# A two-layer graph network on one core: the first layer's sort with fp32 messages, summed one-hots and contiguous operands, and x + offset kept in DRAM

## Chip, core and metric

The kernel runs on one core of one Trainium2 chip. The metric is the device time of one execution in microseconds (us). The core's engines are TensorE (PE; its weight loads are shown apart, as PEld), VectorE (DVE), ScalarE (ACT), GpSimd (POOL) and SyncE (SP, which here only issues DMAs). Each works through its own instruction queue in order and waits there on semaphores.

## What is computed

12,500 nodes with 256 features, 200,000 edges (src, dst) sorted by dst, one weight per edge. Layer 0 is an attention layer with 4 heads of 32, layer 1 a message-passing layer; each is followed by a residual and a layer norm.

```
feat      = relu(x @ W + b)                    # two projections: self (4x32), neighbour (4x32)
att_s     = leaky(feat_self . a_self);  att_n = leaky(feat_nei . a_neigh)
msg[e]    = (att_s[src] + att_n[dst]) * weight[e] * feat_nei[dst]
agg       = segment_sum(msg, src)
norm      = per head (32 wide): (f - mean) * scale * rsqrt(var) + offset,  for self and for agg
x1        = layernorm(x + concat(norm(self), norm(agg)))
m[e]      = relu(concat(x1[src], x1[dst]) @ W_msg + b_msg);  agg1 = segment_sum(m, dst)
h         = layernorm(relu(concat(x1, agg1) @ W_upd + b_upd)) * gamma + beta
out       = layernorm(x1 + h)
```

## The kernel before

Three stages follow one another. **Stage 1, the sort** (tasks in `sort_tasks` and `feat_tasks`), takes the edges in 112 groups of 14 tiles of 128. The dst of a group lie in a window of 128 nodes, whose neighbour features are computed beside it; the messages have to be ordered by blocks of 128 src nodes (98 blocks, and one for padding). For a group:

- `hot` (L530, DVE) makes a one-hot A of each edge's block, laid out block by tile; `ranks` (L550, PE) sums it over edges with 14 products of one column, `begins` (L562) makes the prefix over edges with 14 products; `rows`, `shift`, `steps` and `target` (L605) turn the counts into places in the log and row addresses (`reach` builds Z, whose weights `target` reads at every fourth column).
- `place_mm` (L591, L593, PE) lays each edge's place beside a large constant at its block, in three pieces of 5, 5 and 4 tiles; `place_max` (L617, DVE) reduces each to the maximum over blocks, `split` makes row and column of the place, `hot_r`, `hot_q` (DVE) and `goods` (L637, POOL) their one-hots times four values of the edge, and `permute` (L648, PE) orders these with 14 products.
- `rel_keep`, `rel_out`, `rel_in` send the ordered window positions through DRAM and back broadcast to 128 partitions (512 KB), `hot_n` (L668, DVE) makes one-hots of them, and `message` (L677, PE) multiplies these with the features. Since the one-hots are bf16, the features are split into three bf16 parts (`high`, `rest`, `mid`, `low3`) and each product is done three times: 48 a group. `evict` (L684, ACT) copies them out and `scatter` (L690, POOL) writes 4 x 128 rows to the log in DRAM.
- `feat_tasks` also normalises the self half and adds it to x + offset for one block a group. The result stays in SBUF: the low half transposed (`low_t`, L491; yl), the high half as it is (yh), with statistics of the low half (`low_stats`).

**Stage 2** takes the 98 src blocks in turn. Five pieces of the log a block (`log_load`, SP) are scaled by the attention (`log_hot`, L888, four on POOL and one on DVE), and DVE makes 20 one-hots of the src node times the edge weight (L893) from iotac, a ramp in SBUF; PE sums (`log_sum`, L901, 20 products). For batches of four blocks (`spans`) the head norm follows, then the sum with yh, the layer norm's statistics and the projection for layer 1 (`proj_t` to `proj_s`), which goes to DRAM as pd.

**Stage 3** takes the edges in 781 steps of two tiles: POOL gathers rows of pd by src (L1204), PE adds the window's projection (L1241), DVE and ACT form the sum and the relu (L1263, L1265), PE sums by dst (L1282), and per group the update and the norms follow. `store_x1` (L793) writes x1 of a block to DRAM from yl and yh, one block a group.

The order of each engine's instructions is the order in which the program issues them (PE, ACT, DVE and SP are scheduled by hand; POOL's by the framework). In stage 1 a group begins every 8 steps, and each task stands in a list with its step from the group's begin; at each step the tasks due are issued, older groups first. So four groups are under way at once. A tile of a pool has as many buffers as its `bufs` says (2 where none is given for most pools of stage 1), and a writer waits until the reader of its buffer is done.

Of the kernel before, what the change touches and what calls it, by code (L numbers as in the profile page):

```python
# [29 lines left out]
H = 4  # L30
# [51 lines left out]
def kernel(  # L82
# [43 lines left out]
    pd = dram.tile([ROWS, D], FT, name="pd")  # L126

# [11 lines left out]
    yl = consts.tile([P, NB, P], FT, name="yl")  # L139
    yh = consts.tile([P, NB, HD], FT, name="yh")  # L140
    bst = consts.tile([P, NB, 2, 6], FT, name="bst")
# [57 lines left out]
    with ExitStack() as l0:  # L199
        dcp = l0.enter_context(tc.tile_pool(name="dcp", bufs=1))  # L200
        meta = l0.enter_context(tc.tile_pool(name="meta", bufs=2))
        xin = l0.enter_context(tc.tile_pool(name="xin", bufs=3))
        feat = l0.enter_context(tc.tile_pool(name="feat", bufs=2))
        srt = l0.enter_context(tc.tile_pool(name="srt", bufs=2))
        msgp = l0.enter_context(tc.tile_pool(name="msgp", bufs=2))
# [4 lines left out]
        iotab = dcp.tile([P, NBX, GT], BF, name="iotab")  # L210
# [11 lines left out]
        roww = dcp.tile([P, RW], FT, name="roww")  # L222
        quart = dcp.tile([P, 1], FT, name="quart")
# [3 lines left out]
        nc.gpsimd.iota(iotaw, pattern=[[1, GR]], base=0, channel_multiplier=0,  # L227
# [12 lines left out]
        nc.vector.tensor_copy(iotab, iotac[:, 0:NBX, None].to_broadcast([P, NBX, GT]))  # L240
# [103 lines left out]
        def rel_group(g):  # L344
            c, j = divmod(g, GC)
            n = ntile[g]
            sl = slice(g * GT, g * GT + n)
            nc.vector.tensor_scalar(rel[:, sl], rel[:, sl], baseB[:, g:g + 1], None, op0=OP.subtract)
            nc.vector.tensor_single_scalar(em[c][:, 0, j * GT:j * GT + n], rel[:, sl], 1.0, op=OP.add)

# [16 lines left out]
        def feat_tasks(g):  # L367
# [22 lines left out]
            def keep():  # L390
                xT = feat.tile([P, 4, P], FT, name="xT", bufs=1)
                a, z = (0 if ww else 2), (4 if bb else 2)
                nc.scalar.copy(xT[:, a:z].rearrange("p c q -> p (c q)"), st["tp"][:, a * P:z * P])
                st["xT"] = xT

            def offsets():
                st["y"] = feat.tile([P, HD], FT, name="y")
                nc.vector.tensor_tensor(st["y"], xb[g][:, 0:HD], ofb[:, 0:HD], op=OP.add)
                nc.vector.tensor_tensor(yh[:, g, :], xb[g][:, HD:D], ofb[:, HD:D], op=OP.add)
# [18 lines left out]
            def att_mult():  # L418
                st["tm"] = feat.tile([P, D], FT, name="tm", bufs=1)
# [11 lines left out]
            def centre():  # L431
                st["F"] = feat.tile([P, D + H], FT, name="F")
# [13 lines left out]
            def square():  # L446
                st["q"] = feat.tile([P, HD], FT, name="q", bufs=1)
                nc.scalar.activation(st["q"], st["F"][:, 0:HD], AF.Square)


            def high():
                F3[g] = feat.tile([P, 3, HD + H], BF, name="F3")
                nc.scalar.copy(F3[g][:, 0], st["F"][:, HD:])

            def rest():
                st["r"] = feat.tile([P, HD + H], FT, name="r", bufs=1)
                nc.vector.tensor_tensor(st["r"], st["F"][:, HD:], F3[g][:, 0], op=OP.subtract)

            def mid():
                nc.scalar.copy(F3[g][:, 1], st["r"])  # L460

            def low3():
                nc.vector.tensor_tensor(F3[g][:, 2], st["r"], F3[g][:, 1], op=OP.subtract)
# [19 lines left out]
            def put():  # L483
                nc.vector.tensor_tensor(st["y"], st["y"], st["F"][:, 0:HD], op=OP.add)

            def low_stats():
                nc.vector.bn_stats(bst[:, g, 0], st["y"])

            def low_t():
                st["yt"] = ps.tile([P, 512], FT, name="tp")  # L490
                nc.tensor.transpose(st["yt"][:, :P], st["y"], ident)  # L491

            def low():
                nc.scalar.copy(yl[:, g, :], st["yt"][:, :P])
# [5 lines left out]
                    (11, k(square)), (12, w(high)), (12, k(var)), (13, w(rest)), (13, k(root)), (14, w(mid)),  # L500
                    (14, k(rstd)), (14, k(norm)), (15, w(low3)), (15, k(scale)), (15, k(put)),
                    (16, k(low_stats)), (16, k(low_t)), (17, k(low)))
# [13 lines left out]
        def sort_tasks(g):  # L516
# [10 lines left out]

            def hot():
                st["A"] = srt.tile([P, NBX, GT], BF, name="A")
                nc.vector.tensor_tensor(st["A"], iotab, blk[c][:, None, tl].to_broadcast([P, NBX, GT]),  # L530
                                        op=OP.is_equal)

            def twins():
                e = srt.tile([P, GT, GT], BF, name="e", bufs=1)
# [10 lines left out]
            def ranks():  # L545
# [3 lines left out]
                for t in range(GT):  # L549
                    nc.tensor.matmul(st["sm"][:NBX, 0:1], st["A"][:, :, t], onesb,  # L550
                                     start=(t == 0), stop=(t == GT - 1))
# [6 lines left out]
            def begins():  # L558
                r = st["rows"]
                nc.tensor.matmul(st["sm"][:NBX, 1:2], less[:NBX, :NBX], r, start=True, stop=True)  # L560
                for t in range(GT):
                    nc.tensor.matmul(st["V"], lessb, st["A"][:, :, t], start=(t == 0), stop=False)  # L562
# [19 lines left out]
            def reach():  # L582
                nc.vector.tensor_scalar(small("Z", GR, bufs=1), iotaw[:NBX], st["b0"], None, op0=OP.is_ge)

            def place_mm(i):
                def f():
# [6 lines left out]
                    nc.tensor.matmul(o, identk, st["A"][:, :, a:a + n].rearrange("p b t -> p t b"),  # L593
# [9 lines left out]
            def target():  # L603
                for k in range(RW):
                    nc.tensor.matmul(st["sm"][:, 4 + k:5 + k],  # L605
                                     st["Z"].rearrange("b (p k) -> b k p", k=RW)[:, k], st["ds"],
# [5 lines left out]
            def place_max(i):  # L612
                def f():
                    a, n = CH[i]
                    if i == 0:
                        small("sl", GT, p=P)
                    nc.vector.tensor_reduce(  # L617
                        st["sl"][:, a:a + n], st.pop(("w", i))[:, :n * NBX].rearrange("p (t b) -> p t b", b=NBX),
                        AX.X, OP.max)
                return f  # L620

            def split():
                sl = st["sl"]
                q, r, f = small("q", GT, BF, p=P), small("r", GT, BF, p=P), small("f", GT, p=P)
                nc.vector.scalar_tensor_tensor(sl, sl, -BIG, st["d"], op0=OP.add, op1=OP.add)
# [4 lines left out]
            def hot_r():  # L630
                st["rh"] = srt.tile([P, NR, GT], BF, name="rh", bufs=1)
# [3 lines left out]
            def goods():  # L635
                st["mv"] = srt.tile([P, NR, 5, GT], BF, name="mv", bufs=1)
                nc.gpsimd.tensor_tensor(st["mv"], st["rh"][:, :, None, :].to_broadcast([P, NR, 5, GT]),  # L637
                                        em[c][:, None, :, tl].to_broadcast([P, NR, 5, GT]), op=OP.mult)

            def hot_q():  # L640
                st["qh"] = srt.tile([P, P, GT], BF, name="qh", bufs=1)
# [3 lines left out]
            def permute():  # L645
                mv = st["mv"].rearrange("p r m t -> p (r m) t")
                for t in range(GT):
                    nc.tensor.matmul(st["sm"][:, 16:16 + 5 * NR], st["qh"][:, :, t], mv[:, :, t],  # L648
# [18 lines left out]
            def hot_n():  # L667
                nc.vector.tensor_scalar(st["rr"], st["rr"], pcol1, None, op0=OP.is_equal)  # L668
                st["oT"] = st["rr"].rearrange("p (q r) -> p q r", r=NR)

            def message(i):
                def f():
                    r0, n = 3 * i, min(3, NR - 3 * i)
                    mp = st["mp", i] = ps.tile([P, 512], FT, name="mp")
                    for r in range(n):
                        for k in range(3):
                            nc.tensor.matmul(mp[:, r * (HD + H):(r + 1) * (HD + H)], st["oT"][:, :, r0 + r],  # L677
                                             F3[g][:, k], start=(k == 0), stop=(k == 2))
# [9 lines left out]
            def scatter(k):  # L688
                def f():
# [7 lines left out]
                    for p in zeros[-16:] if g >= GZ else zeros[:nz0] if g < 2 else []:  # L697
# [3 lines left out]
            tasks = [(0, lambda: rel_group(g)), (0, hot), (0, twins), (1, ranks), (2, rows), (2, twin_sum),  # L701
                     (3, begins), (4, vhigh), (5, vlow), (5, shift), (5, reach), (6, place_mm(0)), (6, place_mm(1)),
                     (6, steps), (7, place_max(0)), (7, steps_keep), (8, place_max(1)), (8, place_mm(2)),
# [835 lines left out]
```

## Time and profile before

| | us |
|---|---|
| three runs, lowest, median, highest | 5433.82, 5439.74, 5442.79 |
| profiled execution, time | 5431.22 |
| its span, first to last instruction | 5429.4 |
| stage 1, stage 2, stage 3 (of the span) | 0 to 2356, to 3408, to the end |
| busy: PE, weight loads, DVE, ACT, POOL | 4904.7, 4013.7, 3925.2, 1960.4, 2885.6 |
| mean granted clock of TensorE | 0.827 of full speed |

The profile is that of one execution. It gives each engine's busy time (matmuls are pipelined and their ends are modelled, so a busy PE is not a PE at its peak), groups of instructions by source line, a timeline, and for any stretch the clock that TensorE was granted, as a share of full speed. Durations of neighbours on an engine overlap; what an instruction costs its engine is better read from the step between two starts.

### The profile page before, as it was taken

To read this page: it belongs to the slowest core of one execution; us is meant where nothing else is said; L and a number is where in the kernel's file an instruction comes from. 1 tells how busy PE (TensorE), PEld (TensorE's weight loads), DVE (VectorE), ACT (ScalarE), POOL (GpSimd) and SP (SyncE) were. 2 spreads that over 40 slices of the span, in tenths; PEclk is the share of its full clock that TensorE was granted. 3 is DMA by queue.
4 is the path that set the end of the run, shared out by engine and by line. 5 is a ranking of instruction groups with operands and counts; after the bars stand their busy time and mean duration, and the time that the engine had idled before them with its cause. 6 is when DMAs were issued, how large, how long until landed. Compare 5 with 4: busy or idle time off the path is not lost.

```text
span 5429.4 us, 85561 instructions
## 1 busy us (share of the span) xinstructions
PE 4904.7 (90%) x26835; PEld 4013.7 (74%) x26835; DVE 3925.2 (72%) x11063; ACT 1960.4 (36%) x5351; POOL 2885.6 (53%) x2797
## 2 busy tenths in 40 slices
PE   8999999999999999989999999788888888888887
PEld 6777777777777777767777777666667667676665
DVE  6767777666666676579999999666666666666666
ACT  2222222222222222211111111566666666666655
POOL 2333333333333333344544444677777777777776
PEclk7666666666666666689999999999999999999999
DMA  3333333322232222244444445566666666666665
GB/s 111 112 121 114 124 119 114 117 94 93 91 98 87 96 88 90 82 130 134 137 135 135 135 136 142 158 180 175 180 178 176 180 178 177 180 174 181 176 171 139
DMA packets 439071, 738.09 MB, mean 136 GB/s; under 512 B 85828, under 2 KB 272998, under 8 KB 438614
## 3 DMA queue, kind: packets, MB, share of 16 engines
q1 hardware_dynamic: 307878, 388.95, 24.9%
q0 software_dynamic: 110848, 327.87, 19.7%
q10 hardware_dynamic: 19888, 15.74, 0.9%
q8 instruction: 218, 3.57, 0.3%
q14 instruction: 239, 1.96, 0.1%
HBM read 540.59 MB, written 191.70 MB: 135 GB/s over the span
## 4 chain that ended last, share of the span: by engine, by line
PE 54%; DVE 21%; DMA 14%; issue 5%; ACT 3%; POOL 2%; DVEq 0%; POOLq 0%; SPq 0%; ACTq 0%
DMA gb<-pd,srcf 14%; PE sum L901 11%; PE mp L677 7%; PE agg L1282 6%; DVE rr L668 5%; PE wp L593 5%; DVE o L893 4%; PE fs L648 4%; PE wp L591 4%; PE fs L605 3%; PE qp L1241 3%; DVE gb L1263 2%; PE fs L405 2%; ACT gb L1265 2%; POOL gb L1204 2%
## 5 line engine op out<-in xcount | busy, mean ns | idle before, releaser
L1204 POOL DMA_INDIRECT gb<-pd,srcf x1563 | 1508.2, 965 | 500.4 <-issue 225.5
L690 POOL DMA_INDIRECT log<-m,ix x448 | 455.9, 1018 | 1430.9 <-ACT m L684 736.3
L1263 DVE TENSOR_TENSOR gb<-qp,gb 128x512 f32<-128x512 f32 x781 | 538.8, 690 | 661.8 <-DMA gb<-pd,srcf 519.0
L1282 PE MATMUL agg<-gb,o 128*128 128x256 f32 x3126 | 877.8, 405 | 125.6 <-ACT gb L1265 120.6
L901 PE MATMUL sum<-lg,o 120*128 120x256 f32 (+1 forms) x3920 | 918.0, 387 | 68.8 <-DVE o L893 56.1
L901 PEld LDWEIGHTS sum<-lg,o 120*128 120x128 f32 (+1 forms) x3920 | 739.0, 192 | 215.5 <-DVE o L893 91.0
L893 DVE TENSOR_SCALAR o<-iotac,lg 120x128 f32<-120x128 f32 (+1 forms) x1960 | 802.3, 478 | 48.0 <-PE sum L901 34.3
L1282 PEld LDWEIGHTS agg<-gb,o 128*128 128x128 f32 x3126 | 586.1, 198 | 315.3 <-ACT gb L1265 239.9
L1265 ACT ACTIVATE gb<-gb 128x512 f32<-128x512 f32 x781 | 490.4, 628 | 727.2 <-DVE gb L1263 724.1
L888 POOL TENSOR_TENSOR lg<-lg 120x512 f32<-120x512 f32 x392 | 449.1, 1152 | 483.3 <-DMA lg<-log 246.9
L677 PE MATMUL mp<-F,rr 128*128 128x132 bf16 x5376 | 569.9, 271 | 44.6 <-DVE rr L668 39.2
L677 PEld LDWEIGHTS <-rr 128*128 128x128 bf16 x5376 | 532.3, 163 | 66.5 <-DVE rr L668 57.8
L1241 PE MATMUL qp<-qh,oT 128*128 128x256 f32 x1563 | 550.4, 373 | 7.3 <-DMA dr<-in_dst_dram 7.3
L684 ACT COPY m<-mp 128x396 f32<-128x396 f32 (+1 forms) x672 | 303.8, 453 | 698.4 <-PE mp L677 698.2
L1241 PE MATMUL qp<-ql,oT 128*128 128x256 f32 x1563 | 415.1, 287 | 0.0
L593 PE MATMUL wp<-A,identk 128*128 128x495 bf16 x336 | 335.4, 998 | 0.0
L1241 PEld LDWEIGHTS qp<-qh,oT 128*128 128x128 f32 x1563 | 308.4, 197 | 32.0 <-DVE oT L1228 7.5
L1241 PEld LDWEIGHTS qp<-ql,oT 128*128 128x128 f32 x1563 | 308.9, 198 | 17.9
L668 DVE TENSOR_SCALAR rr<-rr,pcol 128x2048 bf16<-128x2048 bf16 x112 | 316.5, 2826 | 5.3 <-DMA rr<-reld 5.3
L617 DVE TENSOR_REDUCE sl<-wp 128x5 f32<-128x495 f32 x336 | 212.5, 632 | 137.7 <-PE wp L593 137.7
L562 PE MATMUL fs<-A,lessb 128*128 128x99 bf16 x1568 | 299.1, 357 | 0.0
L831 PE MATMUL qm<-wms,xT 128*128 128x256 f32 x224 | 90.4, 490 | 227.2 <-ACT xT L826 227.0
(244 smaller groups left out, 8616.4 us busy)
## 6 DMA issues: line engine op xcount, KB each, us to landing
dr<-in_dst_dram SPq DMA_DIRECT2D x781, 128.0 KB
lg<-log SPq DMA_DIRECT2D x392, 251.2 KB
rr<-reld SPq DMA_DIRECT2D x112, 512.0 KB
log<-zero SPq DMA_DIRECT2D x101, 268.0 KB
lg<-log SPq DMA_DIRECT2D x98, 268.0 KB
gb<-pd,srcf POOLq DMA_INDIRECT x1563, 4.0
xw<-in_x_dram SPq DMA_DIRECT2D x112, 128.0 KB
xw<-x1d SPq DMA_DIRECT2D x112, 128.0 KB
```

The lines of the kernel that those rows point to most:

```text
L593: nc.tensor.matmul(o, identk, st["A"][:, :, a:a + n].rearrange("p b t -> p t b"), start=False, stop=True)
L668: nc.vector.tensor_scalar(st["rr"], st["rr"], pcol1, None, op0=OP.is_equal)
L677: nc.tensor.matmul(mp[:, r * (HD + H):(r + 1) * (HD + H)], st["oT"][:, :, r0 + r], F3[g][:, k], start=(k == 0), stop=(k == 2))
L690: ins = nc.gpsimd.indirect_dma_start(out=log[:, :], out_offset=bass.IndirectOffsetOnAxis(ap=st["ix"][:, k:k + 1], axis=0), in_=st["m"][:, ...
L888: e.tensor_tensor(t[:n, 1, :, 0:HD].rearrange("p r (h k) -> p r h k", h=H), t[:n, 0, :, 0:HD].rearrange("p r (h k) -> p r h k", h=H), t[:n ...
L893: nc.vector.tensor_scalar(o[:n, r], iotac[:n], t[:n, 0, r, MW - 2:MW - 1], t[:n, 0, r, MW - 1:MW], op0=OP.is_equal, op1=OP.mult)
L901: nc.tensor.matmul(sums[b], o[:n, r], t[:n, :, r, 0:HD], start=(k == 0 and r == 0), stop=(k == NK - 1 and r == RW - 1))
L1204: nc.gpsimd.indirect_dma_start(out=gb[s][:r, i], out_offset=None, in_=pd[:, :], in_offset=bass.IndirectOffsetOnAxis(ap=srci[:r, t:t + 1], ...
L1241: nc.tensor.matmul(qp[:r, i], oT[:, i * P:i * P + r], q, start=(k == 0), stop=(k == 1))
L1263: nc.vector.tensor_tensor(z, qp, z, op=OP.add)
L1265: nc.scalar.activation(z, z, AF.Relu)
L1282: nc.tensor.matmul(agg[g], o[:r, i], z[:r, i], start=(j == 0 and i == 0), stop=lastmm)
```

## The change

In stage 1:
- The one-hot A is laid out tile by block, from a copy of the block numbers that ACT widens first (`widen`); DVE adds its 14 tiles to 4 (`halves`, C), and `ranks` and `begins` use C with 4 products each. `place_mm` reads A contiguously.
- `place_max` goes from DVE to ACT: 14 activations a group, relu of the value less the constant, summed over blocks by the activation's accumulator.
- `reach` fills Z so that `target` reads contiguous weights; `goods` lays mv out so that `permute` streams contiguous columns.
- `hot_n` writes fp32 one-hots to a tile of its own, and `message` is one fp32 product instead of three bf16; the split of the features goes.
- Both halves of x + offset + norm(self) go to DRAM (`out_y`, yd); the transposes, copies and statistics of stage 1 for it go.
- More buffers, and steps moved by one to three.

In stage 2 y is loaded from DRAM a batch at a time (`load_y`), the statistics are over all 256 columns, `proj_t` transposes both halves, and x1 is written here (`store_x1`, ACT and SP) instead of in stage 3. The one-hots of L893 read their ramp from PSUM (iotap), and the log is loaded 9 pieces ahead instead of 4, with 12 buffers instead of 7.

```diff
-                for t in range(GT):
-                    nc.tensor.matmul(st["sm"][:NBX, 0:1], st["A"][:, :, t], onesb,
-                                     start=(t == 0), stop=(t == GT - 1))
+                for i, v in enumerate(st["C"]):
+                    nc.tensor.matmul(st["sm"][:NBX, 0:1], v, onesb, start=(i == 0), stop=(i == 3))
...
+            def widen():
+                st["bx"] = srt.tile([P, GT, NBX], BF, name="bx")
+                nc.scalar.copy(st["bx"], blk[c][:, tl, None].to_broadcast([P, GT, NBX]))
+            def halves():
+                A = st["A"]
+                C = srt.tile([P, 7, NBX], BF, name="C")
+                nc.vector.tensor_tensor(C, A[:, 0:7], A[:, 7:14], op=OP.add)
+                nc.vector.tensor_tensor(C[:, 0:3], C[:, 0:3], C[:, 3:6], op=OP.add)
+                st["C"] = [C[:, i] for i in (0, 1, 2, 6)]
...
-                    nc.tensor.matmul(o, identk, st["A"][:, :, a:a + n].rearrange("p b t -> p t b"),
+                    nc.tensor.matmul(o, identk, st["A"][:, a:a + n],
...
-                                     st["Z"].rearrange("b (p k) -> b k p", k=RW)[:, k], st["ds"],
+                                     st["Z"][:, k * P:(k + 1) * P], st["ds"],
...
-                    nc.vector.tensor_reduce(
-                        st["sl"][:, a:a + n], st.pop(("w", i))[:, :n * NBX].rearrange("p (t b) -> p t b", b=NBX),
-                        AX.X, OP.max)
+                    w = st.pop(("w", i))
+                    for k in range(n):
+                        nc.scalar.activation(small("junk", NBX, BF, p=P), w[:, k * NBX:(k + 1) * NBX], AF.Relu,
+                                             bias=nbig, accum_out=st["sl"][:, a + k:a + k + 1])
...
-                st["mv"] = srt.tile([P, NR, 5, GT], BF, name="mv", bufs=1)
+                st["mv"] = srt.tile([P, GT, NR, 5], BF, name="mv")
...
-                nc.vector.tensor_scalar(st["rr"], st["rr"], pcol1, None, op0=OP.is_equal)
+                oT = srt.tile([P, P * NR], FT, name="oT")
+                nc.vector.tensor_scalar(oT, st["rr"], pcol1, None, op0=OP.is_equal)
...
-                        for k in range(3):
-                            nc.tensor.matmul(mp[:, r * (HD + H):(r + 1) * (HD + H)], st["oT"][:, :, r0 + r],
-                                             F3[g][:, k], start=(k == 0), stop=(k == 2))
+                        nc.tensor.matmul(mp[:, r * (HD + H):(r + 1) * (HD + H)], st["oT"][:, :, r0 + r],
+                                         F3[g][:, HD:], start=True, stop=True)
...
+            def out_y():
+                nc.sync.dma_start(yd[g * P:(g + 1) * P, :], st["y"])
...
+        iotap = ps.tile([P, P], FT, name="iotap", bufs=1)
+        nc.vector.tensor_copy(iotap, iotac)
...
-                nc.vector.tensor_scalar(o[:n, r], iotac[:n], t[:n, 0, r, MW - 2:MW - 1], t[:n, 0, r, MW - 1:MW],
+                nc.vector.tensor_scalar(o[:n, r], iotap[:n], t[:n, 0, r, MW - 2:MW - 1], t[:n, 0, r, MW - 1:MW],
...
+        def load_y(q):
+            b, n = spans[q]
+            ys[q] = bw.tile([P, BB, D], FT, name="y", bufs=3)
+            nc.sync.dma_start(ys[q][:, :n], yd[b * P:(b + n) * P, :].rearrange("(b p) w -> p b w", p=P))
...
-        LA = 4
+        LA = 9
```

In the step list of a group, `widen` stands at -3, `hot` and `halves` at -1 (`hot` was at 0), the last placement piece, `target`, `index` and `split` one or two later, `hot_r`, `goods`, `hot_q` at 12 (10), `permute` at 15 (13), `rel_out`, `rel_in` at 17 and 19 (15, 17), `hot_n` at 22 (20), the messages at 24 to 29 (21 to 26), their evictions one step behind, the scatters at 27 to 31 (24 to 28).

## Prediction, made before the result was known

> **What bounds the kernel now.** First the page's busy shares, then the stretches of the three stages: the sort of the first layer (0 to 2356 us), the sums over the log (to 3408), the second layer (to the end). In the answer by stretches the columns are the span of the stretch, busy time with counts of PE, weight loads, DVE, ACT and POOL, the granted clock, the DMA share and GB/s.
>
> ```profile
> PE 4904.7 (90%) x26835; PEld 4013.7 (74%) x26835; DVE 3925.2 (72%) x11063; ACT 1960.4 (36%) x5351; POOL 2885.6 (53%) x2797
> ```
>
> ```profile
> 0.00:2356.00 2356.00, 2280.27 (x14055) 1827.37 (x14055) 1602.03 (x4849) 577.21 (x1929) 869.73 (x793) 0.65 0.31 103
> 2356.00:3408.00 1052.00, 984.25 (x4390) 823.82 (x4391) 1004.89 (x2432) 131.22 (x366) 507.68 (x441) 0.97 0.48 136
> 3408.00:5429.00 2021.00, 1640.17 (x8392) 1362.47 (x8390) 1318.23 (x3783) 1251.99 (x3057) 1508.16 (x1563) 0.95 0.62 174
> ```
>
> The sort is bound by PE (97%) at a clock of 0.65; the log sums by DVE (96%) with PE right behind (94%). The second layer follows POOL: its timeline there is gathers of 0.95 us with 0.30 us between, one per 1.25 us; 1563 of them are 1954 of the 2021 us. So I read the sort by PE's timeline over one group (start us, us, engine, line; xN merges N instructions, and an fp32 product counts as two):
>
> ```profile
> 1000.50 0.87 PE L593 MATMUL wp<-A,identk 128*128 128x396 bf16 x1
> 1001.19 1.80 PE L605 MATMUL fs<-ds,Z 99*128 99x1 f32 x8
> 1002.86 0.74 PE L677 MATMUL mp<-F,rr 128*128 128x132 bf16 x9
> 1003.43 2.60 PE L550 MATMUL fs<-onesb,A 128*99 128x1 bf16 x14
> 1005.90 0.51 PE L677 MATMUL mp<-F,rr 128*128 128x132 bf16 x3
> ...
> 1007.29 2.67 PE L562 MATMUL fs<-A,lessb 128*128 128x99 bf16 x14
> ...
> 1011.85 2.27 PE L648 MATMUL fs<-mv,qh 128*128 128x80 bf16 x14
> 1013.94 1.17 PE L677 MATMUL mp<-F,rr 128*128 128x132 bf16 x9
> ...
> 1018.42 1.14 PE L405 MATMUL fs<-w0s,xT 128*128 128x128 f32 x8
> 1019.40 1.29 PE L677 MATMUL mp<-F,rr 128*128 128x132 bf16 x18
> ```
>
> From the first line to its next appearance at 1020.98 a group takes 20.48 us. I price by the step from one start to the next, since ends overlap. Two things are to be seen. An operand with a stride costs by the column: L593 streams 396 strided columns in 0.69 us, where L591 beside it streams 396 contiguous ones in 0.17; L562 takes 0.178 us for 99, L648 0.149 for 80, each 1.7 to 1.9 ns a column. And the clock, in stretches of 2 us, is 1.00 from 1018 to 1002 of the next group and 0.50 from 1004 to 1016: it falls behind L605 and L550, 22 products of one column that leave the array almost idle.
>
> **The sort, part by part (PE, us per group, at full clock).**
> - Counts (L550): 14 strided loads, 2.47, become 4 contiguous ones. L598 loads 99 contiguous columns twice in 0.13, so 4 x 0.065 = 0.26.
> - Prefix products (L562): 2.49 becomes 4 of 99 columns, 0.25 by L677's 0.57 for nine.
> - One-hot products of the placement (L593): 0.69 + 0.89 + 0.87 = 2.45 becomes 0.17 + 2 x 0.21 = 0.59.
> - Permutation (L648): 2.09 becomes 14 x 0.063 = 0.88; its weights stay strided, but L677's bf16 weights are strided too and pass at 0.063.
> - Targets (L605): 1.67 for 8 strided loads becomes 8 x 0.084 = 0.67 (L598's load scaled to 128 columns).
> - Messages: 48 bf16 products, 3.96, become 16 fp32, that is 32 instructions. Streaming 132 columns at L405's rate (0.98 us for 8 of 128) is 0.12 us or less, but their weights are fp32 and strided, and the nearest row is L605: 1.67/8 = 0.209 us a load. Taken: loads bound them, 32 x 0.209 = 6.7. From below 32 x 0.125 = 4.0 (L405's contiguous loads). From above, load and stream in series, 32 x 0.32 = 10.2. So messages get dearer, by 2.7.
> - The rest, unchanged but now at full clock: other placement products 1.18 (1.97 now), transposes 0.43 (0.85), L560 and L563 0.42 (1.31 with a wait of 0.47), L598 0.13, projection 0.98; the transpose of y goes (0.11).
>
> Sum: 6.7 + 0.26 + 0.25 + 0.59 + 1.18 + 0.88 + 0.67 + 0.43 + 0.42 + 0.13 + 0.98 = 12.5 against 20.48. The quiet run of 22 one-column products (4.1 us beside 0.57 of messages) shrinks to 12 in 0.9 us with messages between, so I take the clock as mostly full.
>
> [...]
>
> **The other engines of the sort now matter.** DVE is busy 14.4 us of a group. Away go the three maxima (L617, 1.8), the bf16 split of the messages (0.55), the statistics (0.2) and one of two adds (0.2). L668's one-hot takes 0.74 us alone but 3.49 mostly: it ends 0.55 us after POOL's L637 (2.26 us). Alone, with fp32 out, I put it between 0.74 and 2.1 (2048 elements at the 1.0 ns that lies between L617's two shapes, 666 and 565 ns for 495 and 396), at 1.2. Added: two half-sums of 693 and 297 elements, 0.7 to 1.2 by L530 (0.79 for 1386) and its double. That is 10.4 to 10.9, and 13 if one instruction still waits out L637, as a tiny one (L440) did for 2.82 us late in the sort. The new order of mv's elements changes L637's reads; I keep its price.
>
> ACT is busy 5.2 us and gains most: widening 1386 elements (L1265: 512 in 628 ns; L416: 256 in 418; so 1.3 us) and 14 activations of 99 columns that also sum. L1249, with a bias, takes 0.34 us a step for 128; the sum's readout appears nowhere, so from 0.31 (nothing for it) to 0.55 (a small ACT step of 0.24 more), taken 0.45: 6.3. Less three copies (0.8), ACT stands at 9.5 to 12.9, taken 11.5.
>
> PE 12.5, ACT 11.5, DVE up to 13, each in order, with two buffers between: this is no longer one bound. A ring shows it. The placement sums wait for PE's products; behind them in ACT's queue stand the group's rs copy (it waits for the permutation, and the trip through DRAM behind it), the steps copy, for which PE's targets wait, and the message evictions, for which PE's next message waits. By the steps above ACT reaches its first placement sums some 1.1 us later in a group than PE has them, and PE pays that at a message. With 1.4 more for DVE's waits and remaining half-clock windows I take **15.0 us a group**.
>
> SP gains one wait: the store of y (128 KB) waits for DVE's last add two steps earlier; behind it stand rr's load and the next x. rr's own trip, issue at 2344.36 to its one-hot at 2348.67 with DMA quiet, is 4.3 us plus 1.5 for the write before; seven steps of 1.9 us are there for it. DMA is at 0.31 of the sort; the same bytes and 128 KB more in 15/20.7 of the time make about 0.45. The -BIG constant, iotaw's order and the mask of the last rows are work ahead of the loop or in one group: nothing.
>
> First to last L668 is 55.4 to 2348.7, 111 steps of 20.66 us. Gain: 111 x (20.66 - 15.0) = 628 us.
>
> **The log sums.** A block takes 10.64 us. DVE's 20 one-hots (L893) average 478 ns in rows of 331 to 1427; the long ones wait out POOL's L888 (1.05).
>
> ```profile
> 2805.37 3.93 DVE L893 TENSOR_SCALAR o<-iotac,lg 120x128 f32<-120x128 f32 x4
> ```
>
> Here four take 3.93 us while POOL runs two products; free of it twelve take 4.62 with POOL busy at both ends. With the ramp in PSUM, L571's and L413's rows (99 in 0.25, 256 in 0.43, PSUM in) give 0.28 us, 20 x 0.28 = 5.6; if the lock does not mind, nothing is won. With the batch's steps DVE needs 8 to 9. PE then bounds: 40 x 0.216 (24 in 5.18) + 4 x 0.216 + two transposes 0.22 = 9.7. ACT's x1 stores and SP's y loads hide (ACT is at 12%), the x1 stores on SP with nine loads of lead behind them instead of four. I take 10.0: 98 x 0.64 = 63 us, bounds 0 and 92.
>
> **The second layer** loses, per group of 18 us, a transpose, two activations and a store beside POOL's gathers: 0 to 20 us, taken 10.
>
> **Sum** against the profiled execution (5431.2 us, span 5429.4): 5431 - 628 - 63 - 10 = **4730 us**. The runs' median is 0.16% above it; 0.2% is about what a measurement here can tell from no change.
>
> **Rivals.**
> - Full overlap: no ring, PE's floor of 12.5 and a bit: 12.9 x 111 gives 4500 us; if loads cost by column only, DVE's 13 takes over at the same place. For it: PE is fed without a break now. Against: ACT's load doubles. 0.17.
> - ACT takes over: at 0.75 us a sum, 5.2 + 14 x 0.75 = 15.7 and waits, 16.8 a group: 4930. No row bounds the readout from above. [...] 0.16.
> - Load and stream in series, or the clock still half for 13 of 20 us (since load-bound messages fill the array only half of the time): PE 16, with waits 17: 4950. 0.17.
> - Slower: a 64-byte stride of fp32 weights costs more than L605's 16-byte one. PE without messages is 5.8; break-even is at 20.66 + 73/111 = 21.3 us a group, messages 15.5, 0.485 us a load, 3.8 ns a column against 1.63. At 4.5 ns: 24.2 a group, 5750 us. The 28-byte strides of L550 and L562 (1.78, 1.80) speak against. 0.05.
> - The fewer products bring nothing, since the ring locks at the old period: 5360 us. 0.02.
>
> My forecast (4600 to 4860) has 0.43. Faster 0.94, same 0.01, slower 0.05. The range: 4490, for the floor, to 4990, for the half clock.
>
> **What would show it.** Per group: messages of 6.7 us in 32 steps of 0.209; counts 0.26; clock above 0.85 in the sort; ACT busy over 70% there; L893's long rows gone. Message steps far from 0.209, or ACT's sums far from 0.45, would make the number wrong.

## The result and the profile after

The changed kernel takes **4726.06 us** (median of 4 runs, 4723.41 to 4726.86) where the kernel before takes 5438.06 us (4 runs on the same chip, 5433.82 to 5442.79): ratio **0.869, 95% interval 0.8675 to 0.8705**. The forecast was 4730 us. The profiled execution's span is 4724.1 us, 705.3 less than before.

First the page's line of busy shares, then the answer by stretches for the sort (first to last `hot_n`, L659), the log sums (first to last sum, L876) and the second layer, in the columns explained above.

```profile
PE 4094.3 (87%) x22705; PEld 3495.8 (74%) x22705; DVE 3744.7 (79%) x10534; ACT 2522.8 (53%) x8179; POOL 3062.8 (65%) x2797
```

```profile
46.00:1727.00 1681.00, 1493.19 (x9759) 1338.15 (x9759) 1545.46 (x4180) 1113.76 (x4751) 1046.14 (x766) 0.95 0.44 147
1746.00:2697.00 951.00, 950.98 (x4478) 826.24 (x4478) 834.97 (x2429) 192.71 (x450) 482.61 (x439) 1.00 0.63 174
2712.00:4724.00 2012.00, 1604.10 (x8256) 1296.77 (x8256) 1316.51 (x3757) 1178.83 (x2849) 1510.84 (x1563) 0.98 0.62 169
```

The clock of the sort rose from 0.65 to 0.95, and the engine that is nearly always busy is no longer PE (89%) but DVE (1545 of 1681, 92%). In the log sums PE has taken DVE's place at 100%. The second layer is as it was, paced by POOL.

| us | before | after | gain | forecast |
|---|---|---|---|---|
| sort, per group (111 steps between first and last `hot_n`) | 20.66 | 15.14 | 5.52 | 5.66 |
| sort | 2293.3 | 1681.1 | 612 | 628 |
| log sums, per block (98) | 10.63 | 9.70 | 0.93 | 0.64 |
| log sums | 1042 | 951 | 91 | 63 |
| second layer | 2008 | 2012 | -4 | 10 |

The rest of the 705 us is the start, 9 us shorter up to the first `hot_n`, less 3 us in the gaps between the stages.

Now one group. This is the changed kernel's PE timeline; the bracket at a line's end is PE's idle time ahead of it and what the profile holds to have ended it.

```profile
1000.82 1.94 PE L667 MATMUL mp<-F,oT 128*128 128x132 f32 x8
1002.60 0.37 PE L578 MATMUL wp<-vh,identb 128*128 128x495 bf16 x1
...
1003.65 0.37 PE L580 MATMUL wp<-A,identk 128*128 128x495 bf16 x1
1005.47 0.30 PE L585 MATMUL fs<-dl,step 99*99 99x1 f32 x2 [1.45 <-ACT junk L606]
...
1007.53 2.86 PE L667 MATMUL mp<-F,oT 128*128 128x132 f32 x12
1010.23 0.33 PE L578 MATMUL wp<-vh,identb 128*128 128x396 bf16 x1
```

From step to step the twelve message instructions take 2.70 us, 0.225 each; 32 of them are some 7.1 us a group. PE's only large pause is ahead of the steps product L585. Over the whole sort it comes to 142 us, by the list of waits (us in total, times, longest), while the page's group of the messages has 4.2 us of idle time:

```profile
PE fs L585 <- ACT junk L606: 94.6, 65, 1.5
...
PE fs L585 <- DVE dl L563: 47.3, 36, 1.9
```

```profile
L667 PE MATMUL mp<-F,oT 128*128 128x132 f32 x3584 | 880.2, 394 | 4.2 <-DVE v L459 1.4
```

The name of ScalarE's placement sums (L606) misleads. L585 reads dl (DVE, `shift`), and in all 103 pauses of over 0.1 us that the sort's records have ahead of it, it starts 0.145 to 0.147 us after the end of L563, which writes dl. DVE's and POOL's timelines show why dl was late.

```profile
1001.54 0.15 DVE L562 TENSOR_TENSOR dl<-pos,b 99x1 f32<-99x1 f32 x1
1001.72 3.60 DVE L563 TENSOR_TENSOR dl<-dl,capc 99x1 f32<-99x1 f32 x1
1005.25 0.15 DVE L564 TENSOR_TENSOR pos<-pos,rows 99x1 f32<-99x1 f32 x1
```

```profile
1002.21 3.09 POOL L625 TENSOR_TENSOR mv<-rh,em 128x1120 bf16<-128x1120 bf16 x1
```

An addition of one column takes 3.60 us instead of 0.15, and it ends as POOL's goods product L625 does (1005.30). In other groups L562 is the one that waits; of the 108 runs of the two lines that take over 0.5 us, 107 end 14 to 29 ns after an L625. Over the sort the two lines take some 3.2 us a group more than their shortest; so much of DVE's 13.9 busy us is, by this reading, a wait for POOL, and the experiments have to show it.

### The profile page after: what moved, and what is told of

Same layout as the page of the kernel before. It is cut to its first block, busy times and chain, and to the rows that moved or that the text cites. A ratio compares the mean times of both kernels' runs of the same rounds, so it can differ in the third digit from the quotient of the medians.

```text
span 4724.1 us, 79669 instructions
## 1 busy us (share of the span) xinstructions
PE 4094.3 (87%) x22705; PEld 3495.8 (74%) x22705; DVE 3744.7 (79%) x10534; ACT 2522.8 (53%) x8179; POOL 3062.8 (65%) x2797
## 4 chain that ended last, share of the span: by engine, by line
PE 45%; DVE 23%; DMA 17%; ACT 7%; issue 5%; POOL 4%; DVEq 0%; SPq 0%; ACTq 0%; POOLq 0%
PE sum L876 18%; DMA gb<-pd,srcf 16%; PE mp L667 8%; PE agg L1274 5%; DVE dl L563 4%; POOL gb L1196 4%; DVE gb L1255 3%; DVE dl L562 3%; ACT gb L1257 3%; DVE oT L659 2%; PE qp L1233 2%; PE fs L592 2%; PE qm L964 2%; DVE A L512 1%; DVE Z L570 1%
## 5 line engine op out<-in xcount | busy, mean ns | idle before, releaser
L680 POOL DMA_INDIRECT log<-m,ix x448 | 520.1, 1161 | 623.4 <-ACT m L674 332.9
L876 PE MATMUL sum<-lg,o 120*128 120x256 f32 (+1 forms) x3920 | 880.2, 378 | 9.8 <-POOL lg L863 9.8
L667 PE MATMUL mp<-F,oT 128*128 128x132 f32 x3584 | 880.2, 394 | 4.2 <-DVE v L459 1.4
L667 PEld LDWEIGHTS mp<-F,oT 128*128 128x128 f32 x3584 | 819.5, 311 | 8.3 <-ACT m L674 2.2
L876 PEld LDWEIGHTS sum<-lg,o 120*128 120x128 f32 (+1 forms) x3920 | 733.0, 189 | 114.2 <-POOL lg L863 10.0
L868 DVE TENSOR_SCALAR o<-iotap,lg 120x128 f32<-120x128 f32 (+1 forms) x1960 | 656.4, 400 | 115.6 <-PE sum L876 107.7
L606 ACT ACTIVATE junk<-wp,nbig 128x99 bf16<-128x99 f32 x1568 | 520.7, 359 | 11.6 <-PE wp L580 3.3
L625 POOL TENSOR_TENSOR mv<-rh,em 128x1120 bf16<-128x1120 bf16 x112 | 355.6, 3175 | 6.6 <-DVE rh L620 3.7
L606 ACT ACTIVATION_READ_ACCUMULATOR junk<-wp,nbig 128x1 f32 x1568 | 342.1, 218 | 0.0
L1220 DVE TENSOR_SCALAR oT<-dr,baseP 128x256 fp32r<-128x256 int32 x782 | 288.8, 369 | 11.2 <-DMA dr<-in_dst_dram 11.2
L1241 ACT ACTIVATE o<-iotac,rel 128x128 f32<-128x128 f32 x782 | 266.0, 387 | 1.5 <-issue 1.5
```

The source lines that it names most:

```text
L606: nc.scalar.activation(small("junk", NBX, BF, p=P), w[:, k * NBX:(k + 1) * NBX], AF.Relu, bias=nbig, accum_out=st["sl"][:, a + k:a + k + 1])
L625: nc.gpsimd.tensor_tensor(st["mv"], st["rh"].rearrange("p r t -> p t r")[:, :, :, None].to_broadcast([P, GT, NR, 5]), em[c][:, :, tl].rear ...
L680: ins = nc.gpsimd.indirect_dma_start(out=log[:, :], out_offset=bass.IndirectOffsetOnAxis(ap=st["ix"][:, k:k + 1], axis=0), in_=st["m"][:, ...
L868: nc.vector.tensor_scalar(o[:n, r], iotap[:n], t[:n, 0, r, MW - 2:MW - 1], t[:n, 0, r, MW - 1:MW], op0=OP.is_equal, op1=OP.mult)
L876: nc.tensor.matmul(sums[b], o[:n, r], t[:n, :, r, 0:HD], start=(k == 0 and r == 0), stop=(k == NK - 1 and r == RW - 1))
```

## Experiments

After the result two theories stood. **DVE theory:** DVE's chain with its wait for POOL's goods sets the sort's period. **Ring theory** (the prediction's): the placement sums on ScalarE stand late in its queue, and PE pays. A third question is what each part of the change is worth alone. Every edit below starts from the changed kernel. "Period" is us a group in the sort; PE, DVE and ACT are busy us a group; "before" is the kernel before on the same chip: the median of 4 runs in the first row, of 7 in the last, one run in the others. The changed kernel and the last one have 4 runs each, the experiments between them one each. Where "before" is 5789 or 5827 the second layer of every kernel traced there took some 350 us longer, so I compare the stages.

| run | period | PE | DVE | ACT | clock | total | before |
|---|---|---|---|---|---|---|---|
| changed kernel | 15.14 | 13.5 | 13.9 | 10.0 | 0.95 | 4726 | 5438 |
| e1_shift | 14.70 | 13.5 | 13.5 | 10.1 | 0.94 | 5053 | 5827 |
| e2_goods_dve | 13.95 | 13.1 | 12.8 | 10.1 | 0.99 | 4973 | 5827 |
| e3_bf16 | 14.67 | 10.9 | 13.7 | 10.2 | 0.84 | 5054 | 5827 |
| e4_bf16_goods | 14.55 | 11.0 | 12.6 | 10.2 | 0.84 | 5037 | 5827 |
| no_sums | 14.29 | 13.9 | 11.8 | 10.0 | 0.98 | 4977 | 5789 |
| max_dve | 16.27 | 13.4 | 15.4 | 5.6 | 0.88 | 5204 | 5789 |
| goods_order | 17.69 | 14.6 | 12.4 | 10.0 | 0.78 | 5366 | 5789 |
| bf16_goods_order | 16.15 | 12.5 | 12.4 | 10.2 | 0.73 | 5196 | 5789 |
| goods_mid_iota | 15.59 | 14.0 | 13.1 | 10.0 | 0.88 | 4848 | 5428 |
| contig_la4 | 15.64 | 11.6 | 14.8 | 9.9 | 0.86 | 4777 | 5428 |
| no_sums_goods | 14.17 | 14.0 | 11.8 | 10.1 | 0.98 | 4612 | 5428 |
| no_sums_goods_contig | 13.43 | 11.4 | 12.6 | 9.8 | 0.94 | 4530 | 5439 |

**e1_shift**: the small steps of `shift` no longer read two SBUF tensors each.

```diff
-                nc.vector.tensor_tensor(dl, pos, st["b0"], op=OP.subtract)
-                nc.vector.tensor_tensor(dl, dl, capc[:NBX], op=OP.add)
+                nc.vector.scalar_tensor_tensor(dl, st["sm"][:NBX, 1:2], -1.0, pos, op0=OP.mult, op1=OP.add)
+                nc.vector.tensor_scalar(dl, dl, capc[:NBX], None, op0=OP.add)
```

(pos and mx likewise.)

> The four small steps of shift (dl, pos, mx) read at most one tensor from SBUF each: the count from PSUM, the others as a scalar by pointer. Two theories on what bounds the changed sort at 15.1 us a group. Lock: DVE is the bound, since 3.4 us of its group are L562 and L563 waiting out POOL's goods (3.2 us); PE's 1.5 us of idleness before the steps product follows from it. PE: the strided fp32 loads of the messages (7.1 us) and the ring through ACT's placement sums bound it. [...] If PE's idleness there is a cost of its own: 13.7 us a group, 4565 us. If the ring through ACT: nothing changes, PE still idles 1.5 us before steps, 4725 us.

PE's pause ahead of L585 is gone, though ScalarE does the same work as before, and the period falls by only 0.44, to 14.70, which lies in the DVE theory's range of 14.6 to 15.2: the wait moved to the next instruction that was not rewritten. This is the group of e1_shift's Z (`reach`), which takes 0.48 where nothing holds it; the columns are busy us, mean ns and idle time.

```profile
L570 DVE TENSOR_SCALAR Z<-iotaw,b 99x512 f32<-99x512 f32 x53 | 177.6, 3351 | 0.0
```

The rewritten pos and mx take 0.20 us in every group, also in the 39 and 50 groups in which they start while POOL's product runs; Z, like them a tensor_scalar with one tensor in, waits for it and takes 3.35 us on average. So the number of tensors read from SBUF does not by itself tell which instruction waits, and what else does, no run shows.

**e2_goods_dve**: the goods product goes from POOL to DVE (`nc.gpsimd.tensor_tensor` becomes `nc.vector.tensor_tensor`, nothing else).

> goods (mv, 1120 elements) moved from POOL to DVE. [...] If lock: DVE falls by 3.4 - 1.2 = 2.2 us a group, PE's idleness before steps goes, and PE's own 13.5 us bounds: 13.5 to 14.0 us a group, 4540 to 4600 us. If PE or the ring through ACT bounds: no gain, 15.1 us or up to 1 more, 4720 to 4830 us.

```profile
46.00:1595.00 1549.00, 1453.36 (x9762) 1331.74 (x9760) 1419.60 (x4293) 1121.44 (x4762) 711.05 (x655) 0.99 0.47 160
```

Although DVE takes over 2.16 us of work (1.2 were expected, at a price per element that no run shows), its busy time falls from 13.9 to 12.8 and the period by 1.19. PE is now busy 94% of the period and its clock 0.99. The wait for POOL was worth over 1 us a group, as the DVE theory has it.

**max_dve**: ScalarE's 14 placement sums become DVE's three maxima again.

> The changed kernel with the sum readout of the placement given back to VectorE (three tensor_reduce of 0.63 us, from the kernel before, in place of 14 activations of 0.32 us on ScalarE). If VectorE's chain sets the period: 15.14 + 1.9 = 16.6 to 17.1 us, ScalarE's share falling from 66% to about 35%. If the ring through ScalarE's readout (TensorE waiting for it ahead of the steps) sets it: 14.2 to 15.1, and those waits gone.

```profile
48.00:1854.00 1806.00, 1489.33 (x9757) 1355.38 (x9758) 1704.70 (x4510) 626.44 (x1681) 1054.24 (x766) 0.88 0.40 137
```

ScalarE falls to 35% busy and the sort is 1.13 us a group slower, with DVE at 94%. That is a little under the DVE theory's 16.6 to 17.1, and far from the ring theory's 14.2 to 15.1: with ScalarE all but free PE idles 2.9 us a group instead of 1.7, and 282 us of that in the sort ahead of the permutation, for POOL's goods product. With e1_shift, where the pause went while ScalarE's work stayed, the ring theory falls.

**e3_bf16 and e4_bf16_goods**: the messages as three bf16 products a tile again, with the split of the features; e4 has goods on DVE as well.

```diff
-                        nc.tensor.matmul(mp[:, r * (HD + H):(r + 1) * (HD + H)], st["oT"][:, :, r0 + r],
-                                         F3[g][:, HD:], start=True, stop=True)
+                        for k in range(3):
+                            nc.tensor.matmul(mp[:, r * (HD + H):(r + 1) * (HD + H)], st["oT"][:, :, r0 + r],
+                                             F3[g][:, k], start=(k == 0), stop=(k == 2))
```

> The messages alone go back to three bf16 products (48 a group, with the split of the features on ACT and DVE, one-hots in bf16); all else as changed. PE's messages should take 48 x 0.063 = 3.0 us instead of 7.1 at full clock. DVE: the split adds 0.55, the bf16 one-hot takes 0.75 instead of 1.27: the same sum. If PE bounds: 15.1 - 4.1 = 11 and DVE's sum then, some 14 us a group: 4600 us or less. If lock (DVE): nothing gained, 14.8 to 15.4 us a group, 4690 to 4750 us, with PE busy under 75% in the sort.

> Both: messages in three bf16 products and goods on DVE. PE 9.4 us of work a group, DVE 11.8 without the lock, ACT 10.5. If lock: the two gains add beyond either alone, 12 to 13 us a group, 4370 to 4490 us. If PE alone bounded: as the bf16 run alone. If the ring through ACT: 14 us or more, 4600 us.

In e4 twelve bf16 products take 0.74 us, so 48 are 3.0 us against 7.1 in fp32: the fp32 products cost PE 4 us a group. Yet taking them back is worth 0.47 in e3, for DVE sets the pace, and in e4 nothing: at 14.55 it is slower than e2 (13.95) with 2 us less PE work. That misses the DVE theory's 12 to 13 and would fit the ring's "14 us or more", but PE's pauses in e4 are for DVE's vl (260 us in the sort, against 55 for ScalarE's evictions ahead of messages). Here is e4's PE timeline:

```profile
1003.19 0.37 PE L592 MATMUL wp<-vh,identb 128*128 128x495 bf16 x1
1006.65 0.57 PE L592 MATMUL wp<-vl,identb 128*128 128x495 bf16 x1 [3.09 <-DVE vl L572]
1007.02 0.62 PE L594 MATMUL wp<-A,identk 128*128 128x495 bf16 x1
```

PE has caught up with DVE: vl, DVE's operand for the placement's second product, stands behind goods and hot_q (3.3 us) in DVE's queue. After the pause of 3.09 us a product of 495 columns takes 0.62 instead of 0.37 (0.41 from start to start against 0.21), the granted clock is 0.63 from 1006 to 1008 and 0.51 from 1008 to 1010, and DVE then waits 1.4 us for the projection that PE runs at half speed. So PE and DVE are a ring, and the clock lengthens it.

**no_sums**: the summed one-hots are undone, the contiguous layout of A stays.

```diff
-                for i, v in enumerate(st["C"]):
-                    nc.tensor.matmul(st["V"], lessb, v, start=(i == 0), stop=False)
+                for t in range(GT):
+                    nc.tensor.matmul(st["V"], lessb, st["A"][:, t], start=(t == 0), stop=False)
```

(the counts likewise; `halves` is out.)

> The changed kernel without the one-hots summed over tiles: 14 products instead of 4 for the counts and 14 instead of 4 for the prefix, and VectorE's two adds (0.52 and 0.32 us) gone. Periods are of the sort, from line hot_n's first to its last over 111 steps; the changed kernel has 15.14. TensorE there is busy 13.45 us of a group and VectorE 13.9. If the sums are what brought TensorE's work below VectorE's chain: 20 products more at 0.18 to 0.21 us are 3.6 to 4.2 us, TensorE 17.0 to 17.7, period 17.3 to 18.2. If VectorE with its wait sets the period whatever TensorE does: 15.1 less the 0.84 us, 14.3 to 15.1.

The sums were not what brought PE's work down: without them the sort is **faster**, by 0.85 us a group, at the low end of what the second alternative gives.

```profile
44.00:1630.00 1586.00, 1546.17 (x11938) 1438.29 (x11938) 1311.47 (x3964) 1106.82 (x4753) 1086.99 (x766) 0.98 0.46 156
```

DVE's busy time falls by 2.1 us a group, 0.84 of them the adds and the rest waiting, and PE, busy 97%, now sets the period. Its timeline shows why PE can bear the 20 products more:

```profile
1003.03 0.81 PE L542 MATMUL fs<-A,lessb 128*128 128x99 bf16 x14
1003.68 0.43 PE L543 MATMUL fs<-less,rows 99*128 99x99 f32 x2
```

Fourteen products that stream contiguous columns take 0.65 us, 0.046 each. The same fourteen streaming strided columns took 2.49 before. That was at half clock, but at full clock they would take 2.4, by the 1.74 ns a column of the L593 of before (396 strided columns in 0.69 us), which is an estimate. The fourteen counts, whose weights are now contiguous, take 0.64 instead of 2.47. The gain ascribed to fewer products was mostly the layout's; the sums themselves save some 0.9 us of PE's time (counts and prefix 0.39 instead of about 1.3) and cost 0.84 of DVE's, which was the bound.

**goods_order and bf16_goods_order**: e2 and e4 with hot_r, goods and hot_q listed behind vl of the next group, and all that follows two steps later.

```diff
-                     (10, target), (10, place_max(2)), (11, index), (11, split), (12, hot_r), (12, goods), (12, hot_q),
-                     (15, permute), (16, rel_keep), (16, extras), (17, rel_out), (19, rel_in), (22, hot_n)]
+                     (10, target), (10, place_max(2)), (11, index), (11, split), (14, hot_r), (14, goods), (14, hot_q),
+                     (17, permute), (18, rel_keep), (18, extras), (19, rel_out), (21, rel_in), (24, hot_n)]
```

> Goods on VectorE, and hot_r, goods and hot_q listed two steps later (with all that follows them), so that vl, dl and Z of the next group stand ahead of them in VectorE's queue. Goods on VectorE alone had 13.95 us a group, TensorE busy 13.1 of it and idle 0.95 us ahead of the vl product. If TensorE is the bound once that wait is gone: 13.1 to 13.5. If the wait merely moves (to hot_q's readers or to the messages): 13.8 to 14.3.

> The same with the messages as three bf16 products again. Without the reordering this had 14.55 us a group, TensorE busy 11.0, VectorE 12.65, TensorE idle 3.1 us ahead of the vl product and the granted clock 0.85. If the order in VectorE's queue was the cause: VectorE's 12.65 us becomes the bound, period 12.7 to 13.3, clock back to 0.93 or more. If it was not: 14.2 to 14.8 and clock 0.85.

Both missed, and the fault is in the edit: `extras` of a group (DVE's reading of its ordered goods, m) now stands behind `ranks` of the second next one (step 17), which takes the same PSUM bank. In goods_order's PE timeline the counts wait, and what follows runs at a clock of 0.50; below it, the same stretch in windows of 2 us (busy, clock, DMA share, GB/s).

```profile
1010.99 0.50 PE L538 MATMUL fs<-onesb,C 128*99 128x1 bf16 x4 [3.17 <-DVE m L648]
1011.36 1.67 PE L667 MATMUL mp<-F,oT 128*128 128x132 f32 x6
1012.82 1.71 PE L592 MATMUL fs<-ds,Z 99*128 99x1 f32 x8
```

```profile
1006.00:1008.00 2.00, 1.82 (x20) 1.00 0.55 203
1008.00:1010.00 2.00, 0.00 (x0) 0.92 0.42 139
1010.00:1012.00 2.00, 1.01 (x7) 0.50 0.23 68
...
1018.00:1020.00 2.00, 2.00 (x11) 0.52 0.34 137
1020.00:1022.00 2.00, 2.00 (x12) 1.00 0.04 8
```

One pause of 3.2 us is followed by some 9 us at half clock: eight targets take 1.56 us to the next start, where they take 0.81 at full clock.

**goods_mid_iota**: the reordering mended (hot_r, goods, hot_q at 13.5, permute at 15.5, extras at 16.5), and in the log sums the one-hots' ramp back in SBUF. **contig_la4**: `hot_n` writes its one-hot so that the messages' weights are contiguous, and the log is loaded 4 pieces ahead as before the change. The stages follow one another, and the log sums took 9.66 or 9.67 us a block, from first to last one-hot, in every run that edits the sort alone, so each run is two experiments.

```diff
-                nc.vector.tensor_scalar(oT, st["rr"], pcol1, None, op0=OP.is_equal)
+                nc.vector.tensor_scalar(oT, st["rr"].rearrange("p (q r) -> p r q", r=NR), pcol1, None, op0=OP.is_equal)
...
-                nc.vector.tensor_scalar(o[:n, r], iotap[:n], t[:n, 0, r, MW - 2:MW - 1], t[:n, 0, r, MW - 1:MW],
+                nc.vector.tensor_scalar(o[:n, r], iotac[:n], t[:n, 0, r, MW - 2:MW - 1], t[:n, 0, r, MW - 1:MW],
...
-        LA = 9
+        LA = 4
```

> Two edits in two stages. Sort: goods on VectorE, with hot_r, goods and hot_q listed behind vl, dl and Z of the next group, and this time permute and extras still ahead of the next counts, so that the bank of the sums is read out in time. Goods on VectorE alone: 13.95 us a group, TensorE busy 13.1, idle 0.95 ahead of the vl product. If that wait is all that is left: 13.1 to 13.5 us. If a wait of over 2 us comes up elsewhere and the clock falls: 14.5 to 17.7, as the two-step reordering did. Log sums: the ramp of the one-hots back in SBUF. If the ramp in PSUM gave the 0.93 us a block: 10.4 to 10.7 us, one-hot at about 480 ns instead of 400. If the deeper look-ahead gave it: 9.7 us, unchanged.

> Two edits in two stages. Sort: hot_n writes its one-hot as 16 by 128, so that the messages' weights lie contiguous (in the changed kernel with a stride of 64 bytes, 0.223 us a product, 7.1 us a group). If the strided weights are the price: 0.12 to 0.16 us a product, TensorE's work 13.45 to 10.3 to 11.5 us a group. If the product's fp32 passes are: 0.21 to 0.23 us, TensorE as before. The period is VectorE's in both: hot_n reads with a stride, 1.27 us becomes 2.1 to 2.6, so 15.9 to 16.6 us instead of 15.14; if TensorE set it, it would fall below 15. Log sums: look-ahead of 4 instead of 9. If the look-ahead gave the 0.93 us a block: 10.4 to 10.7 us; if the ramp in PSUM: 9.7.

Sort: goods_mid_iota missed its 13.1 to 13.5 (15.59). The wait for vl is gone, but the permutation now waits for hot_q (90 us in the sort, in 93 pauses of 2.0 us at most) and the counts for the bank (32 us in 52), and the clock is 0.88. That is the other alternative's time, with many shorter waits in place of one of over 2 us. In contig_la4 a message instruction takes 0.12 us instead of 0.223 (six in 0.76, eight in 0.92 from start to start): the stride was the price. `hot_n` pays for it with 2.13 us instead of 1.27, and DVE, still the bound, makes the period 15.64, just under the range expected. PE's work, 11.6 us at a clock of 0.86, came out just over its range.

Log sums, from first to last one-hot: 10.62 us a block before, 10.43 with the ramp in SBUF and the rest as changed, 9.69 with the short look-ahead, 9.67 in the changed kernel. So the ramp in PSUM is worth 0.76 of the 0.95 us, and beside it the look-ahead is worth nothing; which other part of the change made the 0.19 us no run shows. This is the ramp's one-hot in goods_mid_iota and in the changed kernel (minimum, median and maximum ns), then its line on the changed kernel's page (busy us and mean ns).

```profile
L868 DVE TENSOR_SCALAR o<-iotac,lg x1960: 304/335/1429, 1793.1 to 2815.0; 120x128 f32<-120x128 f32 x196
```

```profile
L868 DVE TENSOR_SCALAR o<-iotap,lg x1960: 373/401/412, 1744.8 to 2692.5; 120x128 f32<-120x128 f32 x196
```

```profile
L868 DVE TENSOR_SCALAR o<-iotap,lg 120x128 f32<-120x128 f32 (+1 forms) x1960 | 656.4, 400 | 115.6 <-PE sum L876 107.7
```

With the ramp in PSUM the typical one-hot is slower (median 401 against 335 ns), but the mean is lower (400 against 495), since the long ones that wait out POOL are gone (maximum 412 against 1429), and DVE now waits for PE.

**no_sums_goods** joins the two edits that helped, and **no_sums_goods_contig** adds contiguous message weights.

> The sort without the summed one-hots (14.29 us a group alone) and with goods on VectorE (13.95 alone). TensorE 13.1 + 0.5 = 13.6 us, VectorE 12.8 - 0.84 = 11.95. If TensorE is the bound and VectorE the source of its idle time: 13.6 to 13.9. If the two gains are the same gain (VectorE freed once): 13.9 to 14.3. If VectorE's 2.1 us of goods in one piece still make TensorE wait over 2 us at another place: above 14.3 and a clock below 0.95.

> No summed one-hots, goods on VectorE, and contiguous weights for the messages. The first two together had 14.17 us a group with TensorE busy 13.98 of it and VectorE 11.8; contiguous weights took 0.09 us off each of 32 products and put 0.9 us on VectorE. So TensorE's work falls to 11.1 us and VectorE's rises to 12.7. If busy time alone counts: VectorE's 12.7 us sets the period, 12.7 to 13.1, and the kernel is 110 to 160 us faster than with the first two. If TensorE, once it has slack, waits in pieces of 2 us or more and its clock falls, as in the bf16 runs and with contiguous weights alone: 13.6 to 14.6 us, clock 0.80 to 0.92, and the 2.9 us less of work bring little or nothing.

The two gains do not add: 14.17 us, PE busy 99% of it, as the second alternative had it. That is 0.2 more than e2 alone, which fits PE as the bound, where the 0.9 us that the sums save it count; from one run each so small a difference is not sure. With PE's work cut by 2.6 us the period falls to 13.43:

```profile
46.00:1537.00 1491.00, 1261.64 (x11944) 1113.61 (x11943) 1395.32 (x4072) 1085.38 (x4763) 795.21 (x655) 0.94 0.50 166
```

This lies between the two expectations: DVE is busy 12.57 of 13.43 us, PE pauses for vl in 79 places (139 us in all, some 1.7 us each, 2.5 at most), and the clock keeps 0.94. The kernel takes **4530.22 us** (4 runs), **0.8331 of before (0.8317 to 0.8345)**, and beats the changed kernel by some 4%.

## Why the prediction was right, point by point

- **The total** (4730 against 4726) is nearer than its terms, and that is luck: the sort fell 16 us short of the forecast gain and the second layer 14, the log sums went 28 over it, and some 6 us came from the start, which the sum left out.
- **PE's work per group**, 12.5: by start-to-start steps in the changed kernel about 13.0 at full clock. Messages 7.1 (6.7 forecast, 0.223 a load against 0.209), counts and prefix 0.39 (0.51), placement 1.77 (1.77), permutation 0.92 (0.88), targets 0.81 (0.67), transposes 0.47 (0.43), projection 0.98 (0.98). The rows of strided loads carried over; contig_la4 showed that the stride is what they price: with contiguous weights a message instruction takes 0.12, with these 0.223.
- **The credit within it**, "14 strided loads become 4 contiguous ones" and the like for the prefix, was right in size, but four fifths of it (3.7 of 4.6 us) are "contiguous". no_sums shows the sums to be a loss in the changed kernel.
- **"PE pays that at a message"**, the ring through ScalarE, failed. PE waits 4.2 us in the whole stage ahead of messages. It pauses ahead of the steps product, 142 us or 1.28 a group, for DVE's dl; e1_shift and max_dve speak against ScalarE. So 15.0 us a group was near 15.14 by luck: the forecast has PE's 12.5 and a ring's 2.5 us, the runs have DVE's 13.9 with its wait for POOL and some 1.2 us in which DVE is idle.
- **DVE, 10.4 to 10.9, and 13 with one wait**: 13.9 measured, of which some 3.2 is the wait. (The terms listed make 10.1 to 10.6.) The wait was foreseen, as one term beside the ring and not as what sets the period, and its size was off at "I keep its price": L637's 2.26 us became 3.09 with the new order of mv. In that order em is read with 252 bytes between neighbours. No run here changes the order alone, so whether the order is the cause of the 37% more was not shown.
- **ScalarE, 0.45 us a sum**: 0.32, at the lower end, and 10.0 us a group against 11.5 (the terms listed make 12.0), so ScalarE is 66% busy and not over 70%. The forecast held such a miss to make the number wrong; it did not, since ScalarE was not the bound. The rival in which ScalarE takes over did not come; max_dve shows, too, that in this kernel such work left on VectorE would cost 1.13 us a group.
- **The clock mostly full** was right (0.95). Its reason, a shorter run of one-column products, holds for their time and not for their number: no_sums has as many as before, 14 and 8, in 0.64 and 0.81 us, and a clock of 0.98. In the traces of the kernel before and of the changed one all changes of the clock lie whole multiples of 3.41 us apart, to within 9 ns, and in their sorts it went with the columns that PE began to stream in the 3.41 us before (those of an fp32 instruction counted twice: 128 of them take 0.123 us, where 495 in bf16 take 0.21). Of 466 such stretches with under 2800 columns 458 (98%) were followed by half clock, of 615 with 3300 or more 599 (97%) by full clock. In the kernel before, the sort's 110 falls came though PE had not paused for 0.1 us in the stretch before; 99 of these stretches held 1200 to 2000 columns. That the columns are the cause, and do not only go with it, no run shows by itself.
- **Log sums, 10.0**: 9.70, which is PE's floor as worked out; the margin above it was not needed. The mechanism, the ramp out of POOL's way ("the lock" of the forecast is DVE's wait for POOL's L888, in one-hots of up to 1427 ns), is shown by goods_mid_iota for 0.76 us of the gain. The one-hot's price was off, 0.32 us a step against 0.28, which cost nothing, as PE is the bound there.
- **The second layer, 10 us less**: 4 us more, which at 0.2% is no change. POOL's gathers pace it (1983 us from first to last before, 1986 after), and work taken from beside them was worth nothing.

## What to carry to other kernels

Separate "fewer" from "contiguous" when a product gets cheaper: here the layout gave the gain, and the extra work for fewer products was a loss on the engine that had become the bound. After a change that frees one engine, read the next engine's longest tiny instruction; here an addition of 3.6 us, 0.16 at its shortest, was a wait. Cutting PE's work paid only while what was left kept PE streaming (e4 has 2 us less of it than e2 and is 0.6 slower): a pause of about 3 us was followed by up to 9 us at half clock, and in the kernel before slow strided and one-column products went with the half clock (0.50 from 1004 to 1016) though PE had not paused.

## What was not expected of the hardware

- **The clock after a pause, and without one.** Pauses of 3.09 us (e4) and 3.17 us (goods_order) were followed by half clock for some 3 and 9 us; pauses of 1.7 to 1.8 us in no_sums_goods_contig were mostly not (79 for vl in its sort, 44 falls, clock 0.94), yet in no_sums one of 1.17 us was (0.50 from 1008 to 1010). So the length of the pause alone did not tell whether the clock would fall, and in the kernel before it fell 110 times in the sort with no pause of 0.1 us ahead.
- **The wait for POOL moves.** With dl's steps freed of it, it appeared at Z (3.35 us), and only moving POOL's product ended it. On DVE that product took 2.16 us, on POOL 3.09.
- **The sum's readout** is an instruction of its own: in 800 us of the changed kernel's sort 728 activations of 358 ns are followed by 728 readouts of 218 ns, yet a pair takes only about 0.32 us from start to start, so the two overlap.
